# Layer 3's norm taken by halves of the channels, with a first job that begins on the upper half, and another order in layer 0's opening

## The chip, the cores and the metric

The kernel runs on one core of a Trainium2 chip. The metric is the device time of one launch in microseconds (us), the median of several runs. All data is float32.

## The reference

An image of 1024 channels and 64 x 64 pixels (one batch element) passes four residual layers, each on a group norm of its input (32 groups of 32 channels):

```python
x = x + L0(_gn(x))   # per channel: layer norm over the pixels, then a scan along the channels
x = x + L1(_gn(x))   # 1x1 convolution: weight (1024 x 1024) @ x + bias
x = x + L2(_gn(x))   # three 1x1 projections with silu, a depthwise convolution, two selective scans
                     # along sorted pixel orders, y * silu(gate) + res, an output projection, silu
x = x + L3(_gn(x))   # 1x1 convolution: weight @ x + bias
```

Layer 0, with `xn` the layer norm of its input over the pixels of each channel: `dt = softplus(sum over columns of xn * dt_w + dt_b)`, the decay of a row is `exp(-exp(log_A) * dt)`, and `out[t] = decay[t] * out[t-1] + xn[t]` along the 1024 channels. The group norm of a layer needs the mean and variance of all pixels of a group, so no pixel of a layer can be normalized before the last pixel of the layer before is there. It does not need the other channels' statistics.

## The kernel before

Pixels are cut into 8 blocks of 512 (`nb`), channels into 8 tiles of 128 (`ct`). TensorE does the 1x1 convolutions, VectorE takes statistics (`bn_stats` per tile and block, `bn_aggr` over the blocks of a tile), evicts products from PSUM and forms differences, ScalarE normalizes with `activation(Identity, scale, bias)`, POOL (GpSimd) forms sums and differences in SBUF.

A group norm is `moments` (the aggregation) followed by the generator `norm_steps`: a small matmul `pg` that averages the means over the groups, the squared deviations `d` on VectorE, a second small matmul `pv`, then `rsqrt` (Ln and Exp on ScalarE, three steps on VectorE) and the bias. It yields where one engine has to wait for another, so that the caller can put other work there. `finish_of` runs it to its end. Both small matmuls take a PSUM tile of the tag `tp`, of which there are two.

**Layer 0** works in 8 units of 2 channel tiles and half of the pixels (`u`), in 4 chunks of 2 units (one norm for each chunk, `norm_chunk`), and each unit in 4 pieces (`i`, 32 in all). For each piece: `normalize` (ScalarE), `turn_in` (TensorE transposes, evicted with scale and bias by VectorE or ScalarE according to `share`), `row_dt` (TensorE: the sums for dt into the bank `pd`), then `scan` (VectorE), `hand_on` (last column kept for the next channels), `turn_back` (transposes) and `add_up` (VectorE adds into the image and sums). `decay(u, 0..2)` makes the factors `a` of a unit: four activations, one VectorE addition, one activation. `squares` takes the next layer's variance on ScalarE. `unit_stats` takes the input's statistics. All engines follow the order written in the program (`manual_schedule`): an opening by hand, then a loop over the 32 pieces in which pieces are turned in seven ahead (`LEAD`); `todo` says in which iteration which unit's statistics are taken. `make_scores` prepares the pixel scores for the sort that layer 2 needs; it runs on VectorE ahead of the first statistics. `bring` loads the units on SP's queue, `sums` prepares weights on POOL.

**Layer 2's gate and output projections and layer 3** are matrix products in two levels of a Strassen-Winograd scheme: a job (one weight matrix, a pair of pixel blocks) has 7 outer steps `P1` to `P7` of 7 inner products each, 49 products of 8 matmuls. In `two_steps` everything is placed in slots; slot n of a job stands behind its n-th product in each engine's order. The products of two neighbouring outer steps alternate, so a step stretches over 13 slots:

```python
for slot in range(min(at), max(max(at), end + 6) + 1):
    step, i = divmod(slot, 7)
    if i % 2 == 1:
        step -= 1
    if 0 <= step < 7 * len(jobs):
        j, s = divmod(step, 7)
        outer = orders[j][s]
        product(j, outer, ("P1", "P5", "P2", "P4", "P6", "P3", "P7")[i])
    for f in at.get(slot, ()):
        f()
```

`b11`, `b12` are the upper 512 channels of the pair's first and second block, `b21`, `b22` the lower 512; `fetch` loads them on ScalarE's DMA queue, `fill` normalizes them, `comb` makes the differences t1 = b12 - b11, t2 = b22 - t1, t3 = t2 - b11, t4 = b21 - t2, and `inner_sum` the same inside a block on POOL. `SIDES` names the operand of each step: P1 takes b11, P5 t1, P2 b21, P6 t2, P7 t3, P4 t4, P3 b22. The results are C (upper channels, first block), Q (lower, second), V (lower, first) and Z or D (upper, second). `emit` adds each inner product into them, on VectorE or as a copy on ScalarE; products share PSUM banks of the tags `a`, `b7` and `b23`, two banks each. Weights come on SP's queue through `wq` (10 tiles).

Before, there are two calls of `two_steps` with a full norm between them, so the first layer-3 job (order A: P1, P2, P6, ...) begins after the statistics of all channels:

```python
    two_steps([job for pair in range(NP) for job in (("gate", WG, pair), ("out", WO, pair))], norm2, x1_d)
    nc.scalar.preload_act_table_set("natural_log_exp_and_others")
    norm3 = group_norm("gn3")
```

## Time and profile before

| | |
|---|---|
| median of 3 runs | 2768.85 us (2766.1 to 2771.12) |
| profiled execution | 2769.34 us, of which 2767.6 us span |
| granted TensorE clock, mean | 0.981 |
| first scan of layer 0 | 48.65 us from the span's start |
| first product of layer 1 | 229.28 us |
| last layer-2 product begins | 2401.75 us |
| first layer-3 product begins | 2416.68 us |

In a row of the timeline, the first number is the start in us, the second the length; then engine, line of the kernel, operation, the tile written and the tiles read, shape, and how many instructions were merged; in brackets the idle time before and what ended it. PE is TensorE, DVE VectorE, ACT ScalarE, POOL GpSimd, SP the queue that issues loads. A row of the waits gives the total in us, the number of waits and the longest. A row of busy times by stretch gives the stretch, its length, busy us of PE, PE's weight loads, DVE, ACT and POOL with the number of instructions, the granted clock, the share of the DMA engines and GB/s.

### The profile page before, as it was taken

The numbers are of one execution on the slowest core, as the hardware profiler recorded it, in microseconds if no ns is written. First come the engines' busy times: TensorE is split into PE (matmuls) and PEld (weight loads), VectorE is DVE, ScalarE is ACT, GpSimd is POOL, SyncE is SP. The second block draws the span as 40 slices with busy tenths as digits, with TensorE's granted clock in tenths as the row PEclk, the third lists the DMA queues.
The fourth block names the chain that finished last, engine by engine and source line by source line (L and its number), as shares of the span: only waits on it lengthen the run. The fifth ranks groups of instructions, "written<-read, shape, count | busy, mean of one in ns | idle before, by whom it ended". The sixth has DMA issues, their size and how long they took to land.

```text
span 2767.6 us, 30985 instructions
## 1 busy us (share of the span) xinstructions
PE 2617.4 (95%) x9586; PEld 1728.1 (62%) x9586; DVE 1771.5 (64%) x3773; ACT 1089.5 (39%) x1838; POOL 1300.5 (47%) x1175
## 2 busy tenths in 40 slices
PE   5778999999999999999999999999999999799998
PEld 4564444444555555444444446888888888688887
DVE  6986866464454564466666565577575676767777
ACT  4783110104655654465757554322233132221220
POOL 4154323421213002467686864565565566454544
PEclk9998999999999999999999999999999999899999
DMA  7345467735533434677777876889899898788896
GB/s 283 119 150 196 141 235 249 231 118 192 161 115 101 149 116 110 174 238 221 219 212 215 240 201 192 241 245 292 222 292 266 240 291 232 250 268 296 292 330 213
DMA packets 423578, 591.47 MB, mean 214 GB/s; under 512 B 149973, under 2 KB 211541, under 8 KB 420342
## 3 DMA queue, kind: packets, MB, share of 16 engines
q1 hardware_dynamic: 297110, 362.09, 41.9%
q10 hardware_dynamic: 93568, 140.52, 14.5%
q0 software_dynamic: 32736, 86.88, 12.3%
q8 instruction: 78, 1.28, 0.2%
q14 instruction: 86, 0.70, 0.1%
HBM read 432.02 MB, written 157.36 MB: 213 GB/s over the span
## 4 chain that ended last, share of the span: by engine, by line
PE 49%; POOL 3%; DMA 3%; DVE 3%; issue 1%; ACT 1%; SPq 0%; DVEq 0%; POOLq 0%; ACTq 0%
PE mm L791 9%; PE q_P5P L1547 5%; PE q_P3P L1547 5%; PE q_P7P L1547 5%; PE q_P6P L1547 5%; PE q_P4P L1547 5%; PE q_P1P L1547 5%; PE q_P2P L1547 4%; PE pg L1213 2%; PE py L1230 2%; DMA qD<-x_d 1%; POOL s L430 1%; POOL t L749 1%; PE pr L1189 1%; DMA g<-tok_d,src 0%
## 5 line engine op out<-in xcount | busy, mean ns | idle before, releaser
L791 PE MATMUL mm<-t,w 128*128 128x512 f32 x1536 | 682.8, 595 | 0.0
L791 PE MATMUL mm<-b,w 128*128 128x512 f32 x1152 | 516.9, 600 | 5.4 <-ACT b L875 4.8
L791 PEld LDWEIGHTS mm<-t,w 128*128 128x128 f32 x1536 | 286.3, 190 | 326.2 <-issue 320.7
L791 PEld LDWEIGHTS mm<-b,w 128*128 128x128 f32 x1152 | 217.4, 192 | 257.4 <-issue 246.8
L1516 ACT COPY qQ<-q_P5P 128x512 f32<-128x512 f32 x48 | 28.1, 586 | 328.1 <-PE q_P5P L1547 321.8
L980 DVE SCALAR_TENSOR_TENSOR cvp<-xs,par,cvp 128x512 f32<-128x512 f32 x128 | 95.4, 754 | 84.2 <-ACT cvp L977 81.9
L1007 POOL TENSOR_TENSOR acc<-l2xt,acc 128x136 f32<-128x136 f32 x56 | 27.8, 496 | 246.8 <-ACT l2xt L1001 243.5
L430 POOL TENSOR_TENSOR s<-s 128x256 f32<-128x256 f32 (+3 forms) x120 | 128.7, 1079 | 7.8
L1344 ACT ACTIVATE qb<-x_x_b,gn_bias,gn_r_r 128x512 f32<-128x512 f32 x128 | 96.8, 805 | 82.6 <-DVE qQ L1479 32.3
L1239 POOL DMA_INDIRECT y_d<-y,dst x74 | 75.1, 1014 | 114.4 <-ACT y L1235 48.3
L1233 ACT COPY g<-py 8x512 f32<-8x512 f32 x146 | 83.8, 574 | 111.1 <-PE py L1230 109.7
L1221 DVE TENSOR_TENSOR E<-E,pg 128x512 f32<-128x512 f32 x74 | 50.8, 687 | 109.9 <-PE pg L1213 105.2
L749 POOL TENSOR_TENSOR t<-b,t 128x512 f32<-128x512 f32 x72 | 94.2, 1335 | 55.9 <-DVE t L749 55.8
L889 DVE SCALAR_TENSOR_TENSOR image<-mm,par,image 128x512 f32<-128x512 f32 x64 | 47.2, 746 | 106.6 <-PE mm L791 106.6
L1031 DVE TENSOR_TENSOR xs<-mm,xs 128x512 f32<-128x512 f32 x64 | 41.7, 684 | 114.8 <-PE mm L791 114.8
L999 PEld LDWEIGHTS l2pt<-both,cv 128*128 128x128 f32 x512 | 77.0, 191 | 35.6 <-issue 25.6
L1547 PE MATMUL q_P1P<-t_b,wq_P1P 128*128 128x256 f32 x384 | 92.2, 385 | 6.6 <-issue 6.6
L1340 POOL TENSOR_TENSOR t_t<-qt 128x512 f32<-128x512 f32 x23 | 29.6, 1288 | 142.1 <-DVE qt L1340 80.6
L1547 PE MATMUL q_P4P<-t_t,wq_P4P 128*128 128x256 f32 x384 | 91.5, 381 | 4.9 <-issue 2.8
L1340 POOL TENSOR_TENSOR t_t<-qt,t_t 128x512 f32<-128x512 f32 x46 | 69.7, 1516 | 51.4 <-DVE qt L1340 51.1
L1547 PE MATMUL q_P2P<-t_b,wq_P2P 128*128 128x256 f32 x384 | 92.2, 384 | 0.0
L875 ACT ACTIVATE b<-image,gnl_bias,gnl_r_r 128x512 f32<-128x512 f32 x48 | 36.8, 808 | 137.4 <-DMA s<-in_w_dram 58.5
(380 smaller groups left out, 5990.1 us busy)
## 6 DMA issues: line engine op xcount, KB each, us to landing
w<-s_d SPq DMA_DIRECT2D x96, 512.0 KB, 4.3
w<-in_w_dram SPq DMA_DIRECT2D x72, 512.0 KB, 3.9
x_x_b<-x_d ACTq DMA_DIRECT2D x32, 1024.0 KB, 6.5
image<-x_d SPq DMA_DIRECT2D x12, 2048.0 KB, 12.0
wq_P6P<-s_d SPq DMA_DIRECT2D x84, 256.0 KB, 4.7
wq_P7P<-s_d SPq DMA_DIRECT2D x84, 256.0 KB, 6.3
wq_P5P<-s_d SPq DMA_DIRECT2D x84, 256.0 KB, 4.8
wq_P3P<-s_d SPq DMA_DIRECT2D x84, 256.0 KB, 4.3
```

Source lines behind the costliest of these rows:

```text
L430: eng.tensor_tensor(out, a, b, ALU.subtract)
L749: eng.tensor_tensor(B[name][k], B[one][k], B[two][k], ALU.subtract)
L791: nc.tensor.matmul(to[o], w[:, k, o * P : (o + 1) * P], B[name][k], start=(fresh and k == 0), stop=(k == KH - 1), skip_group_check=True)
L980: nc.vector.scalar_tensor_tensor(cv, xo[:, at + t : at + t + FB], pcol("dww", 3 * o + t), cv, ALU.mult, ALU.add)
L999: nc.tensor.matmul(pt[:, q * NV : (q + 1) * NV], cv[:, (q0 + q) * P : (q0 + q + 1) * P], both[:, o, :], start=True, stop=True)
L1213: nc.tensor.matmul(pg, bts, cd.rearrange("p s t -> p (s t)"), start=True, stop=True)
L1230: nc.tensor.matmul(py, G2[k % 2], rows.pop(k)[:, :DH], start=True, stop=True)
L1233: nc.scalar.copy(rows[k + 1][h * LC : h * LC + S, :DH], py[h * LC : h * LC + S])
L1239: nc.gpsimd.indirect_dma_start(out=y_d[:, :], out_offset=bass.IndirectOffsetOnAxis(ap=dst_[:, k : k + 1], axis=0), in_=y[:, :], in_offset= ...
L1340: eng.tensor_tensor(to, a, b, ALU.subtract)
L1344: nc.scalar.activation(tile_of(j, name)[:, k], held[j, "x", name][:, k], AF.Identity, bias=norm[1][:, ct : ct + 1], scale=norm[0][:, ct : ...
L1547: nc.tensor.matmul(ps[:, o, :], w[:, k, o * P : (o + 1) * P], rhs[:, k, :], start=(new and o == 0 and k == 0), stop=(k == 1), skip_group_c ...
```

## The change

For layer 3: one call of `two_steps` takes all jobs. The last layer-2 job places, beside its own work, the norm of the upper channels from slot 44 (`begin` is the ScalarE table set and the aggregation of 4 tiles, four steps at 46, 46, 47 and 47, the end at 48) and that of the lower channels from slot 56. `norm_steps` yields once more for it (`finer`). The statistics of Q move from slots 46, 47, 49, 50 to 49 to 52. The first layer-3 job gets the order D, which begins with P1 and P5, the steps that need only upper channels; its fetches, fills, combinations and the results of C move to other slots, and t4 gets a tile of its own.

For layer 0: `make_scores` yields between its steps; 18 of them stay ahead of the statistics, the others go between the steps of the first chunk's norm. The four normalizations of the first unit follow each other, pieces 0 and 1 are evicted by VectorE alone, pieces 1 and 3 are transposed into the banks of the tag `pb`. The statistics of units 2 and 3 and most of the second chunk's norm move ahead of the first scan. In the loop, `decay` 1 and 2 move ahead of `add_up`, and the statistics and norms of later chunks begin one iteration earlier and go on by one step in each.

```diff
+ORDER_D = ["P1", "P5", "P2", "P6", "P7", "P4", "P3"]
...
+        if finer:
+            yield
         pv = ps_tp(f"{name}_pv")
...
-        make_scores()
...
+        scores = make_scores()
...
+        score(18)
         for u in (0, 1):
             unit_stats(u, range(8))
-        finish_of(norm_chunk(0))
-        normalize(0)
-        normalize(1)
-        unit_stats(2, range(8))
-        turn_in(0, (1, 3))
-        normalize(2)
-        turn_in(1, (1, 3))
+        chain = norm_chunk(0)
+        for _ in range(3):
+            next(chain)
+            score(4)
+        finish_of(chain)
+        for n in range(4):
+            normalize(n)
+        unit_stats(2, range(4))
+        turn_in(0, range(4))
+        turn_in(1, range(4), "pb")
...
         row_dt(0)
-        normalize(3)
         turn_in(2, (1, 3))
         row_dt(1)
-        turn_in(3, (1, 3))
+        turn_in(3, (1, 3), "pb")
         row_dt(2)
+        unit_stats(2, range(4, 8))
+        unit_stats(3, range(4))
         row_dt(3)
-        unit_stats(3, range(4))
         decay(0, 0)
         normalize(4)
+        unit_stats(3, range(4, 8))
+        chain = norm_chunk(1)
         decay(0, 1)
         decay(0, 2)
+        next(chain)
         normalize(5)
         turn_in(4, ())
+        next(chain)
         row_dt(4)
+        next(chain)
...
-                9: [(7, range(4))], 10: [(7, range(4, 8))], 11: [(6, range(4))], 12: [(6, range(4, 8))]}
+                8: [(7, range(4))], 9: [(7, range(4, 8))], 10: [(6, range(4))], 11: [(6, range(4, 8))]}
...
             if i == 0:
-                unit_stats(3, range(4, 8))
-                finish_of(norm_chunk(1))
+                finish_of(chain)
+                chain = iter(())
+            if g == 3 and u + 1 < NU:
+                decay(u + 1, 1)
+                decay(u + 1, 2)
             if i > 0:
                 add_up(i - 1)
...
-            if i in (4, 12):
-                chain = norm_chunk(2 if i == 4 else 3)
-            if i in (6, 14):
-                finish_of(chain)
+            if i in (3, 11):
+                chain = norm_chunk(2 if i == 3 else 3)
             next(chain, None)
...
+        orders[turning - 1 : turning + 1] = ORDER_C, ORDER_D
...
+        def next_norm(s0):
+
+            for row, slot in ((0, 44), (1, 56)):
+                steps = {}
+
+                def begin(row=row, steps=steps):
+                    nc.scalar.preload_act_table_set("natural_log_exp_and_others")
+                    steps[0] = norm_steps(f"gn3_{row}", *moments(f"gn3_{row}", row * KH, KH), KH, finer=True)
...
+                then(s0 + slot, begin)
+                for i in (2, 2, 3, 3):
+                    then(s0 + slot + i, go_on)
+                then(s0 + slot + 4, end)
...
-                for name, row, col, slot, when in (("b11", 0, 0, -25, -14), ("b12", 0, 1, -14, -3),
-                                                   ("b21", 1, 0, -10, -1), ("b22", 1, 1, 1, 8)):
+                for name, row, col, slot, when in (
+                        (("b11", 0, 0, -7, -1), ("b12", 0, 1, -3, 2), ("b21", 1, 0, 3, 11), ("b22", 1, 1, 8, 14))
+                        if order is ORDER_D else
+                        (("b11", 0, 0, -25, -14), ("b12", 0, 1, -14, -3), ("b21", 1, 0, -10, -1), ("b22", 1, 1, 1, 8))):
                     on(slot, fetch, src_d, pair, row, col, (j, "x", name))
                     for k in range(KH):
-                        on(when + k, fill, j, name, row, col, k)
+                        on(when + (k // 2 if when == -1 and order is ORDER_D else k), fill, j, name, row, col, k)
...
+                if order is ORDER_D:
+                    late = [(2, "t1", "b12", "b11"), (16, "t2", "b22", "t1"), (20, "t3", "t2", "b11"), (27, "t4", "b21", "t2")]
+                    put_in = {0: -1, 1: 5, 2: 13, 3: 19, 4: 24}
...
-                done = (("C", 0, 0, {0: 27, 1: 28, 2: 29, 3: 30}), ("Q", 1, 1, {2: 46, 3: 47, 0: 49, 1: 50}),
+                done = (("C", 0, 0, {0: 27, 1: 28, 2: 29, 3: 30}), ("Q", 1, 1, {2: 49, 3: 50, 0: 51, 1: 52}),
...
-        two_steps([job for pair in range(NP) for job in (("gate", WG, pair), ("out", WO, pair))], norm2, x1_d)
-        nc.scalar.preload_act_table_set("natural_log_exp_and_others")
-        norm3 = group_norm("gn3")
-    with tc.manual_schedule(engines={E_.DVE, E_.PE, E_.Pool, E_.Activation}):
-        two_steps([("last", W3, pair) for pair in range(NP)], norm3, x2_d)
+        two_steps([job for pair in range(NP) for job in (("gate", WG, pair), ("out", WO, pair))]
+                  + [("last", W3, pair) for pair in range(NP)], norm2)
```

## The prediction

> **What bounds the kernel now.** I read the page first, then the chain of waits, then the two places that the diff touches: the seam between the last layer-2 job and the first layer-3 job (chain and PE timeline), and layer 0 (who VectorE waited for, and busy time by stretch).
>
> ```profile
> span 2767.6 us, 30985 instructions
> PE 2617.4 (95%) x9586; PEld 1728.1 (62%) x9586; DVE 1771.5 (64%) x3773; ACT 1089.5 (39%) x1838; POOL 1300.5 (47%) x1175
> PE   5778999999999999999999999999999999799998
> ```
>
> TensorE is the bound almost everywhere. Its row of tenths has two holes: the first four slices (layer 0, some 230 us) and one slice near the end. In the hole near the end the chain of waits leaves TensorE:
>
> ```profile
> 2378.75 1.74 PE q_P7P L1547 x8
> ...
> 2391.47 0.61 DVE qD L1483
> ...
> 2410.50 1.90 DVE gn_mv L179 x8
> ...
> 2415.61 0.18 DVE gn_bias L211
> ...
> 2418.88 1.27 POOL t_b L1340
> ...
> 2425.38 3.69 PE q_P1P L1547 x16
> ```
>
> For 45 us the end is set by VectorE: evictions, residual adds, statistics, then the whole norm of layer 3, and only then the first operand fill. The same place on TensorE:
>
> ```profile
> 2390.67 1.89 PE L1547 MATMUL q_P4P<-t_t,wq_P4P 128*128 128x256 f32 x8
> 2394.64 1.99 PE L1547 MATMUL q_P4P<-t_t,wq_P4P 128*128 128x256 f32 x8 [2.08 <-DVE qV L1524]
> 2399.41 2.55 PE L1547 MATMUL q_P4P<-t_t,wq_P4P 128*128 128x256 f32 x8 [2.77 <-issue]
> 2401.75 3.04 PE L1547 MATMUL q_P4P<-qQ,wq_P4P 128*128 128x256 f32 x8
> 2412.44 0.60 PE L193 MATMUL gn_pg<-gn_mv,cst 128*128 128x8 f32 x2 [7.66 <-DVE gn_mv L179]
> 2416.68 5.90 PE L1547 MATMUL q_P1P<-qb,wq_P1P 128*128 128x256 f32 x16 [2.39 <-ACT qb L1344]
> 2425.38 3.69 PE L1547 MATMUL q_P1P<-t_b,wq_P1P 128*128 128x256 f32 x16 [2.80 <-issue]
> ```
>
> A product (8 matmuls) takes 1.73 us in the steady stretch. From 2392.4 to 2425.4, 33.0 us, TensorE finishes five products, 8.6 us of work: 24.4 us are lost here. That is the most that this part can give. In layer 0, VectorE's waits and busy times:
>
> ```profile
> DVE gn_r_t L170 <- ACT gn_r_r L168: 8.8, 4, 4.3
> DVE xt L591 <- ACT a L583: 6.4, 6, 2.1
> DVE gn_d L196 <- PE gn_pg L193: 6.1, 2, 5.7
> ...
> 48.60:65.60 17.00, 14.40 (x60) 11.64 (x60) 9.98 (x27) 12.73 (x24) 7.21 (x8) 0.71 0.18 65
> ...
> 149.00:189.00 40.00, 35.03 (x215) 28.70 (x214) 35.92 (x76) 39.08 (x74) 19.26 (x32) 1.00 0.45 159
> 189.00:222.80 33.80, 18.27 (x84) 14.14 (x83) 32.30 (x69) 20.39 (x42) 17.28 (x24) 0.65 0.66 239
> ```
>
> The third and fourth busy columns are VectorE and ScalarE. VectorE is full for most of the layer and at its end; ScalarE is full from 149 to 189. VectorE's waits are the norm's round trips (5.7 for the sums on TensorE, 3.5 and 4.3 for Ln and Exp on ScalarE) and the decay factors `a`. Layer 1 begins when this layer ends, so what is saved here reaches the end.
>
> **The seam, walked through.** Slots are products of 1.73 us; slot 49 of the last layer-2 job is slot 0 of the first layer-3 job. Until slot 44 nothing differs, so the last statistics of D end at 2392.8 as they do now. VectorE's queue then gets four aggregations (eight take 1.97, so 1.0) and is at 2393.8. TensorE has finished slot 46 at 2389.0 and must take the norm's first small matmul next: it waits 4.8 us there, in front of slots 47 and 48. Matmul 0.6, slot 47 until 2396.1, second matmul until 2396.8 (the three small VectorE steps that it needs end at 2396.1, behind slot 45's and 46's evictions), Ln and Exp, four VectorE steps of 0.2, norm of the upper half at 2400.0, two fills of 0.8: the first layer-3 product runs from about 2401 to 2403, where it now starts at 2416.7. Slot 1 (a left-over P4 product) covers 1.7. Slot 2 needs fills 2 and 3, which stand on ScalarE behind the eviction of slot 0, a table load and one Silu: 0.57+1.28+0.72+1.6 after 2403.1, so 2407.3: about 2 us of stall. Slots 3 to 8 then run without a gap until 2418.9. VectorE meanwhile has its old work (16 adds and statistics of Q and V, 10 us) and four combs for t1 (2.8): comb 3 ends at 2420.1, so slot 9 waits 1.2; V's statistics end at 2422.7, four aggregations at 2423.7, and the second norm's first matmul, queued after slot 9, waits 1.8 more. Its scale is there at about 2428.4, the fills of b21 at 2430.6; slot 14, the first product that needs them, starts at 2431.9. Now it starts at 2441.2 (seven products before and seven after it run without a hole). Gain 9.3.
>
> What the walk leaves out is the clock. In the trace, the granted clock after the 7.7 us gap is 0.50 (both norm matmuls and the first P1 product), and after the 2.8 us gap it is 0.77 and then 0.66 (2.55 and 3.04 us for a product of 1.73). The Trainium skill, "TensorE: Matmul & The Clock Gate" (The HAM clock gate), says that the clock halves after an idle window of about 3.4 us and needs as long of work to return. Row and rule differ for the short gap: by the rule alone it should not have slowed anything. They agree that the new 4.8 us wait at slot 46 will: some 3.4 us at half speed, 1.7 us of work lost. It speaks against this change, which puts that wait where TensorE now runs at full clock (without it, 9.3; with it, 7.6). I take it, and for the wait on ScalarE's issue of fetches, which the walk counted at 3 us and the trace shows overlapped now, give back 0.9: **8.5 us**.
>
> The sets of ScalarE: now one switch at 2410.2, after the last Silu. With the norm at slot 44 it is ln/exp, Silu again at slot 49, ln/exp at 56: two more. The trace has 1.28 us for a load; the skill, "ScalarE: Activation LUTs" (What ACT_TABLE_LOAD costs), gives 2.66 with the drain. Only the load in front of slot 2 is on the path: 1.28 is in the walk, by the page's price slot 2 is 1.4 later and the gain 7.1. I stay with the trace: the first activation after 2410.2 waits for VectorE, so the drain is not seen either way; both ends are in the range.
>
> At nothing I cost: Q's move from slots 46-50 to 49-52 (VectorE has D before it), the shorter lead of the fetches (xq has four buffers, fetches land in 6.5 us, b21 is issued near 2413 and needed at 2429; if it came late, each us is a us), the new tile for t4, and the other order of steps in this job: in 2425-2510 VectorE is busy 61.0 of 85 us, POOL 44.3, ScalarE 18.6, and the job does the same products. If that slack were not at the right slots, a hole costs what it lasts. SP's weight loads keep their order and stay ten tiles ahead. Bounds of this part: 2 (TensorE waits for both norms in full, at half clock) and 16 (no wait after the first product).
>
> **Layer 0.** Counted from the first norm's end (27.5). Before it: 16 of 22 score steps stay ahead of the statistics, six and the transpose go into the norm's round trips. Statistics could start near 10.6, not 12.9; but the second unit's block (issued at 4.93, 12.1 us to landing, so 17.0) is used from 17.7, so at most 0.7 is won; the steps put into the chain delay it by about as much (a copy that waits for the score transpose stands before `gn_v`). Net 0, bounds -1 and +1.5.
>
> Then the order. Now: first scan 48.65, second 65.60, with VectorE idle 5.7 us in between. Changed: all four normalizations first (4.9 on ScalarE), pieces 0 and 1 evicted by VectorE (four more evictions of 0.49), two pieces in the "pb" banks, so piece 1's transposes don't wait for evictions. The row sums start 0.8 earlier. But 7.4 us of statistics and the second chunk's norm now stand on VectorE before the first scan: m at 48.9, aggregation until 50, the second matmul of that norm behind piece 4's transposes, the first scan near 53.5 instead of 48.65. In return the norm's last steps follow the first scan at once: second scan near 61.8 instead of 65.6. From there TensorE's turn_back, behind ScalarE's evictions, decides: ScalarE's evictions of pieces 5 to 7 come some 1 us later than now (it waits for m before it may write `a`), so the first add-up comes 1.4 to 3.6 us earlier. I take 2, bounds -4 and +5.
>
> Chunks 2 and 3: the chain starts one iteration earlier and goes one step at a time, so that Ln and Exp lie a whole scan before their use. The 3.5 and 4.3 us go. ScalarE is idle 5 of 20 us around the first and 5 of 15 around the second, so some of it turns into waits for ScalarE: 2.5 and 3. The factors `a`: decay steps 1 and 2 move ahead of add-up and evictions. Of 6.4 us, the first scan's 1.07 is in the opening; 2.12 lies where ScalarE is full and gains nothing; of the other 3.2 I take half of the 1.48 before 189 and nearly all of the small ones: 1.5 with rounding down. Sum 2+2.5+3+1.5 = 9; ScalarE's full 40 us (149 to 189) must also start earlier for this to count, which it does only as far as TensorE lets it: I take **7.5**, bounds 0 and 13. Shorter layer 0 also pulls together the weight loads at 205-225 (DMA share 0.7 to 1.0), which cover nothing critical: the first layer-1 product waits for the fill.
>
> **Sum.** 7.5+8.5 = 16. The profiled execution took 2769.34 (span 2767.6 and 1.7 around it), so 2753.3; the median of the three runs shown is 0.5 below that: 2752.9, say 2753.
>
> **Rivals.** (1) The seam closes fully: VectorE catches up while TensorE works on the upper half, no second wait. For it: 14 products, 24 us, lie between first product and first need of the lower half. Against: VectorE was 5.3 us behind at slot 44 already. 15+9: 2745. (2) The wait moves instead of going: small matmuls in TensorE's queue wait for VectorE's backlog twice, at half clock. For it: the walk's 4.8 and 1.8. 3+7 = 10: 2759. (3) Layer 0 is ScalarE's: its later start eats what VectorE saves. 0+8: 2761. (4) Slower, one mechanism: the first scan's delay. The second chunk's norm matmul stands behind piece 4's transposes at half clock; if row sums and transposes of pieces 4 to 6 all run at 0.50 (the trace has 0.50 at 51-55), each costs 1.7 more, ScalarE follows, and layer 0 ends 5 us later than now, while the seam gives 2: 2772. It decides from where the second scan comes later than 67.6 (two us over now's 65.6, the seam's lower bound); VectorE's slack speaks against it. (5) It doesn't do what it says: the layer-3 products wait for the lower half all the same, and layer 0 is neutral: 2767.
>
> **Numbers.** Likeliest case 0.50; (1) 0.20; (2) 0.18; (3) 0.07; (4) 0.03; (5) 0.02. A difference under 0.2% (5.5 us) is about what a measurement here cannot tell from none; the border is 2763.3. Faster by more: all of the first two, nearly all of (2) and most of (3), 0.92; within 0.05; slower 0.03. The range takes (1)'s 2745 with 4 us for the bounds of layer 0, and (3) with the page's dearer table loads: 2741 to 2763.
>
> **What would show it.** Right: PE rows near 2376-2430 (shifted by layer 0) where P1 products of the layer-3 job alternate with P4; one gn_pg wait of 4 to 5 us and a second under 2; three table loads; the aggregation as two groups of four; the first-to-second scan gap near 8, not 17; no Ln wait over 1 us for VectorE. Wrong: a gap over 5 us before the P2 products of that job, holes inside it, or layer 1 beginning no earlier than 229.

## The result, and the profile after

The changed kernel takes 2760.76 us, the median of 10 runs (2757.49 to 2764.36), beside 2770.47 us for 10 runs of the kernel before: a ratio of 0.9965, 95% interval 0.9955 to 0.9974. That is 9.7 us, where 16 were forecast; the time lies in the range.

From the page of the changed kernel, the span, the busy times and the TensorE row of tenths:

```profile
span 2759.0 us, 31019 instructions
PE 2619.3 (95%) x9590; PEld 1728.2 (63%) x9590; DVE 1777.6 (64%) x3785; ACT 1090.0 (40%) x1838; POOL 1303.5 (47%) x1175
PE   4788999999999999999999999999999999899998
```

The busy time of TensorE is the same within 2 us. The hole near the end has gone from a 7 to an 8: it is shallower, not closed.

**The seam.** TensorE's timeline of the changed kernel, the same place as before:

```profile
2392.25 0.59 PE L194 MATMUL gn_pg<-gn_mv,cst 128*128 128x4 f32 x2 [4.73 <-DVE gn_mv L180]
2392.70 3.76 PE L1620 MATMUL q_P7P<-qC,wq_P7P 128*128 128x256 f32 x8
2396.25 0.43 PE L203 MATMUL gn_pv<-gn_d,cst 128*128 128x4 f32 x2
2396.54 2.27 PE L1620 MATMUL q_P4P<-t_t,wq_P4P 128*128 128x256 f32 x8
2401.09 2.27 PE L1620 MATMUL q_P1P<-qb,wq_P1P 128*128 128x256 f32 x8 [2.29 <-ACT qb L1388]
...
2406.76 2.27 PE L1620 MATMUL q_P1P<-qb,wq_P1P 128*128 128x256 f32 x8 [1.68 <-ACT qb L1388]
...
2420.99 1.56 PE L1620 MATMUL q_P5P<-qb,wq_P5P 128*128 128x256 f32 x6 [1.09 <-DVE qb L1384]
2424.96 0.39 PE L194 MATMUL gn_pg<-gn_mv,cst 128*128 128x4 f32 x2 [2.41 <-DVE gn_mv L180]
2425.21 1.97 PE L1620 MATMUL q_P1P<-t_b,wq_P1P 128*128 128x256 f32 x8
```

Before, TensorE had six waits here, 18.4 us in all, the longest 7.66 us in front of the norm. Now it has five, of 4.73, 2.29, 1.68, 1.09 and 2.41 us, 12.2 in all. The first P1 product begins at 2401.09 where it began at 2416.68, and P1 products of the layer-3 job alternate with left-over P4 products. A full-speed product has a row of 1.89 here (its last end is modelled); the one behind the first wait has 3.76. The chain of waits in the same stretch:

```profile
2391.23 0.97 DVE gn_mv L180 x4
2392.84 3.62 PE q_P7P L1620 x8
...
2403.99 1.28 ACT L1552
2405.28 0.73 ACT qQ L1552
2406.03 0.70 DVE qQ L1554
...
2423.95 0.97 DVE gn_mv L180 x4
```

VectorE still sets the end up to the second aggregation at 2423.95, except for two pieces: the slow product at 2392.84, which the norm's second small matmul stands behind, and the load of the Silu table with one Silu at 2403.99, for which VectorE stands idle 5.84 us.

**Layer 0.** VectorE's waits in the first 225 us, then the busy times of the stretch in which ScalarE was full before, then TensorE's timeline at the start of layer 1:

```profile
DVE low L640 <- PE pb L630: 3.2, 1, 3.2
...
DVE xt L616 <- ACT a L608: 2.2, 3, 1.0
...
DVE gn_r_t L171 <- ACT gn_r_r L169: 0.5, 1, 0.5
```

```profile
149.00:189.00 40.00, 36.26 (x218) 30.67 (x219) 36.21 (x75) 39.52 (x74) 20.36 (x32) 1.00 0.47 171
```

```profile
224.07 16.34 PE L828 MATMUL mm<-b,w 128*128 128x512 f32 x31 [2.39 <-ACT b L912]
```

The 8.8 us of waits for Ln and Exp are 0.5, those for the factors `a` fell from 6.4 to 2.2. New is the wait of the first add-up for TensorE's transposes, 3.2. Layer 1 begins 5.2 us earlier. ScalarE (the fourth busy column) is full from 149 to 189 as it was.

To follow a gain through the execution I use a *lead*: the start of a row of VectorE, less the start of the same row in the profile of before (below zero is earlier). The seam's own gain is the lead of the rows near 2350, ahead of it, less the lead of those near 2500, behind it. For the changed kernel these are -1.59 and -8.57: the seam gained 7.0 us.

### The profile page after: what moved, and what is told of

It reads as the page before. It is cut to its first block, busy times and chain, and to the rows that moved or that the text cites. A ratio compares the mean times of both kernels' runs of the same rounds, so it can differ in the third digit from the quotient of the medians.

```text
span 2759.0 us, 31019 instructions
## 1 busy us (share of the span) xinstructions
PE 2619.3 (95%) x9590; PEld 1728.2 (63%) x9590; DVE 1777.6 (64%) x3785; ACT 1090.0 (40%) x1838; POOL 1303.5 (47%) x1175
## 3 DMA queue, kind: packets, MB, share of 16 engines
q0 software_dynamic: 32736, 86.88, 12.2%
q8 instruction: 78, 1.28, 0.2%
## 4 chain that ended last, share of the span: by engine, by line
PE 50%; DMA 3%; POOL 3%; DVE 3%; issue 1%; ACT 1%; DVEq 0%; POOLq 0%; ACTq 0%
PE mm L828 10%; PE q_P7P L1620 5%; PE q_P5P L1620 5%; PE q_P3P L1620 5%; PE q_P6P L1620 5%; PE q_P4P L1620 5%; PE q_P1P L1620 4%; PE q_P2P L1620 4%; PE pg L1250 2%; PE py L1267 2%; DMA qD<-x_d 2%; DMA g<-tok_d,src 1%; POOL s L457 1%; PE pr L1226 1%; POOL t L786 0%
## 5 line engine op out<-in xcount | busy, mean ns | idle before, releaser
L1620 PE MATMUL q_P5P<-t_t,wq_P5P 128*128 128x256 f32 x384 | 90.8, 379 | 0.0
```

The costliest lines, as they stand in the source:

```text
L1620: nc.tensor.matmul(ps[:, o, :], w[:, k, o * P : (o + 1) * P], rhs[:, k, :], start=(new and o == 0 and k == 0), stop=(k == 1), skip_group_c ...
```

## The experiments

All ratios are against runs of the kernel before on the same chip. In the profile of before, layer 1 begins at 229.28; the kernel with the seam's part alone has the same layer 0 and 227.94, and the changed kernel has 224.07 and 225.07 in two profiles. So a difference of 1 us in that column says little.

| kernel | median us | ratio, 95% interval | layer 1 begins | seam's gain |
|---|---|---|---|---|
| changed | 2760.76 | 0.9965 [0.9955, 0.9974] | 224.07 | 7.0 |
| layer 0's part alone | 2767.94 | 0.9993 [0.9985, 1.0001] | 224.50 | 0.0 |
| seam's part alone | 2764.46 | 0.9982 [0.9973, 0.9991] | 227.94 | 4.9 |
| four fills first | 2761.39 | 0.9969 [0.9959, 0.998] | 224.31 | 3.0 |
| Silu ahead | 2756.0 | 0.9951 [0.9934, 0.9969] | 224.28 | 8.8 |
| norm's steps later | 2756.53 | 0.9954 [0.994, 0.9967] | 224.75 | 8.9 |
| Silu ahead, steps later | 2753.86 | 0.9936 [0.992, 0.9953] | 224.23 | 11.2 |
| the same, joint table set | 2753.19 | 0.9944 [0.993, 0.9957] | 224.44 | 11.8 |
| opening alone (seam changed) | 2761.38 | 0.9972 [0.9962, 0.9982] | 226.32 | 7.7 |
| decays as before | 2763.46 | 0.9975 [0.9964, 0.9986] | 226.25 | 6.8 |
| chains as before | 2762.16 | 0.9978 [0.9971, 0.9986] | 225.18 | 5.3 |
| waits filled | 2761.89 | 0.9967 [0.9954, 0.9979] | 224.73 | 6.7 |
| changed, once more | 2761.76 | 0.9959 [0.9943, 0.9975] | 225.07 | 5.4 |

### The two parts apart

The first kernel has the diff's layer-0 hunks alone (`make_scores` to the loop over the pieces), the second all the others.

> Layer 0's part of the change alone, the seam before layer 3 as in the kernel before. In the changed kernel layer 1 begins 5.2 us earlier, but of that 1.4 us is left when the first product of the last two layers' jobs begins (1686.14 before, 1684.73 changed). Theory A (the lead of layer 0 is partly lost in layer 2's scan stretch, 1116 to 1680, whose chain goes over indirect loads, POOL and weight stores): first product of layer 1 at 224 +- 0.5, time 1 to 4 us below the kernel before (ratio 0.9986 to 0.9996). Theory B (the lead carries in full, the loss in the one profile was chance): 5 us, ratio 0.998. Rival C (all of it is lost there, the stretch keeps its own clock): ratio 1.000, and the first product at 1686.

> The seam's part alone, layer 0 as before. Theory: what the profile shows between the seventh step of the last layer-2 job and the first product on lower channels is the seam's own, 7.0 us (slot 14 at 2432.6 against 2441.2, less the 1.6 us of lead it came with): 7 us below the kernel before, ratio 0.9975, and with theory A of the other run the two parts add up to the measured 9.7 us. Rival: the seam depends on what comes in ahead of it (its waits shift with DMA phase), then 4 or 10 us.

By time, layer 0's part is worth 0.07% (1.9 us, its interval reaches from 4 us to nothing), the seam's part 0.18% (5 us). Together they come to 6.9 of the 9.7 us, which is within the intervals. So less than half of layer 0's 4.8 us at the start of layer 1 (229.28 to 224.50) is seen in this time; added to the seam's part, the same hunks are worth more (0.9982 against 0.9965, 4.7 us). The lead in that profile is -4.8 at 401, -3.8 at 495, -2.5 from 680 to 1080 and -1.7 at 1120.

In the seam alone the waits are those of the changed kernel, but the products are not. TensorE's timeline:

```profile
2395.84 3.76 PE L1586 MATMUL q_P7P<-qC,wq_P7P 128*128 128x256 f32 x8
...
2399.68 2.94 PE L1586 MATMUL q_P4P<-t_t,wq_P4P 128*128 128x256 f32 x8
2404.92 3.66 PE L1586 MATMUL q_P1P<-qb,wq_P1P 128*128 128x256 f32 x8 [2.29 <-ACT qb L1354]
```

The second and third product take 2.94 and 3.66, where the changed kernel's profile has 2.27 and 2.27. The waits add up to 12.15 us against 12.20, yet the seam gains 4.9 instead of 7.0. The size of the clock's loss is thus a term of its own, and the part on why comes back to it. (The 2.27 at 2401.09 does not come from the clock: the granted clock is 1.00 there, and part of the product stands until ScalarE's second fill ends.)

### What holds the 1.68 and 2.41 us waits

Theory V: VectorE's own queue of adds and statistics sets when the second norm begins. Theory S: the order on ScalarE (fills behind table load and Silu) does. First, all four fills of b11 go ahead of Q's Silu:

```diff
-                        on(when + (k // 2 if when == -1 and order is ORDER_D else k), fill, j, name, row, col, k)
+                        on(when + (0 if when == -1 and order is ORDER_D else k), fill, j, name, row, col, k)
```

> The changed kernel with fills 2 and 3 of b11 placed on ScalarE ahead of Q's first Silu and its table load. Theory S (every stall of TensorE at the seam is its own): the 1.68 us wait of the second P1 product goes, 1.5 to 1.7 us faster than the changed kernel (ratio to the kernel before 0.9959). Theory V (VectorE's chain through Q's and V's statistics to the second norm is the bound, and TensorE's early waits are slack): Q's Silu comes 1.5 us later, so VectorE idles 7.3 instead of 5.84 us, the second norm's small matmul waits 1.5 us more than its 2.41 and the time is that of the changed kernel within 0.5 us (0.9965).

From TensorE's timeline:

```profile
2404.43 1.89 PE L1620 MATMUL q_P1P<-qb,wq_P1P 128*128 128x256 f32 x8
...
2414.57 1.56 PE L1620 MATMUL q_P5P<-qb,wq_P5P 128*128 128x256 f32 x6 [0.91 <-DVE qb L1384]
...
2423.34 0.59 PE L194 MATMUL gn_pg<-gn_mv,cst 128*128 128x4 f32 x2 [2.40 <-DVE gn_mv L180]
2423.78 3.76 PE L1620 MATMUL q_P1P<-t_b,wq_P1P 128*128 128x256 f32 x8
```

The 1.68 us wait is gone (the second P1 product has no bracket), a new one of 0.91 has come, and the norm waits 2.40 as before: TensorE arrives earlier and waits for VectorE elsewhere. The time is the changed kernel's. VectorE now stands idle 7.24 us for Q's Silu, as V said; the norm's longer wait that V expected did not come, since TensorE came later itself, slowed by its clock. Then Q's Silu itself goes ahead, so that VectorE need not stand idle for it (Q's Silus at their old places fall away):

```diff
+            def silu_q(j, k, o):
+                c = tile_of(j, "Q")[:, k]
+                nc.scalar.activation(c, c, AF.Silu, bias=pcol("bout", o))
...
+                if order is ORDER_D:
+                    for k in (3, 0):
+                        on(-1, silu_q, j - 1, k, KH + k)
...
-("Q", 1, 1, {2: 49, 3: 50, 0: 51, 1: 52}),
+("Q", 1, 1, {2: 49, 3: 49, 0: 49, 1: 50}),
...
+                    if quick and kind == "out" and name == "Q" and k in (1, 2):
+                        on({2: 48, 1: 50}[k], silu_q, j, k, o)
```

> The changed kernel with the Silu table load and Q's first Silu placed in ScalarE's 1.9 us wait for the end of the first norm, two further Silus right behind the first two fills, and Q's adds and statistics on VectorE from slot 49 to 50. Theory V: VectorE's 5.84 us of idle shrinks to 1 to 2 us, V's statistics end 3 to 4 us earlier, the waits of 1.68, 1.09 and 2.41 us go nearly all: 4 us faster than the changed kernel, ratio to the kernel before 0.995. Theory S: only the first wait (1.68) goes, ratio 0.9959. Rival: the Silu delays the first fill by more than it saves: 0.9965 or above.

TensorE's timeline has three waits left, one of 4.71 at the first group sum and these two:

```profile
2402.29 3.64 PE L1630 MATMUL q_P1P<-qb,wq_P1P 128*128 128x256 f32 x8 [2.29 <-ACT qb L1388]
...
2423.87 0.39 PE L194 MATMUL gn_pg<-gn_mv,cst 128*128 128x4 f32 x2 [2.20 <-DVE gn_mv L180]
```

The waits of 1.68 and 1.09 are gone and 9.2 us are left. The ratio is 0.0014 (3.9 us) under the changed kernel's, though the two intervals overlap. VectorE's idle time for Q's Silu is 0.86 instead of 5.84. This speaks for V: VectorE's queue is what runs late, and the table load in front of its work was part of the reason. But the norm still waits 2.20: what VectorE won, TensorE won too.

### The norm's steps two slots later

```diff
-                for i in (2, 2, 3, 3):
+                for i in (4, 4, 4, 4):
```

> The changed kernel with the steps of both half-norms two and one slots later in the last layer-2 job (go_on counts 4,4,4,4 in place of 2,2,3,3), so that TensorE runs slots 47 and 48 before it waits for the aggregated statistics, and the same for the second norm. Theory C (TensorE's queue and clock: a product that could run stands behind the 4.7 us wait, and the wait halves the clock): the gn_pg wait falls from 4.73 to 1 to 2 us, the first P7P product after it runs at 2 to 2.5 us instead of 3.76, the upper half's norm ends 0 to 1.6 us earlier, and the seam is 1.5 to 3 us shorter: ratio about 0.9957 against the changed kernel's 0.9965, in the profile the first P2 product 1.5 to 3 us earlier counted from the first P1 product's predecessors. Theory V (VectorE's own queue decides when the statistics are there and TensorE's waits only move): the wait shrinks by the two products moved ahead, the waits of 2.29, 1.68, 1.09 and 2.41 grow by as much, and the time is the changed kernel's, 0.9965.

TensorE's timeline:

```profile
2395.28 0.39 PE L194 MATMUL gn_pg<-gn_mv,cst 128*128 128x4 f32 x2 [1.27 <-DVE gn_mv L180]
2399.27 0.59 PE L203 MATMUL gn_pv<-gn_d,cst 128*128 128x4 f32 x2 [3.60 <-DVE gn_d L199]
2402.22 3.78 PE L1620 MATMUL q_P1P<-qb,wq_P1P 128*128 128x256 f32 x8 [2.37 <-ACT qb L1388]
```

Now slots 47 and 48 run ahead of the wait, at full speed. The 4.73 becomes 1.27, but six evictions stand on VectorE between the aggregation and `gn_d`, and TensorE waits 3.60 for that. The second norm finds its statistics there at once and waits 1.03 for its `gn_d`. In all 10.05 us of waits instead of 12.2. The ratio, 0.0011 (3 us) under the changed kernel's, is what C expected, though the two intervals overlap. But the slow product has not gone: it is now the first P1, with 3.78, which C did not expect.

### Both together, and the table set

> Both at once: Q's Silu and its table load ahead of the norm's end (the earlier run: the waits of 1.68 and 1.09 gone, ratio 0.9951) and the norm's steps later (the run beside this one). If the two take different losses away, the gains add: with theory C some 5 us under the changed kernel, ratio 0.994 to 0.995. If VectorE's queue is the one limit behind both, no more than the earlier Silu alone gives: 0.9951.

ScalarE's timeline shows a cost that the Silu put ahead has brought in:

```profile
2394.72 1.28 ACT L168 ACT_TABLE_LOAD   x1
2397.68 0.20 ACT L168 ACTIVATE gn_r_r<-gn_v 128x4 f32<-128x4 f32 x1 [1.67 <-DVE gn_v L211]
2397.90 1.28 ACT L169 ACT_TABLE_LOAD   x1
```

The set loaded for Ln does not hold Exp, so a second load of 1.28 us stands between the two, with VectorE waiting. The next kernel names the joint set behind that Silu:

```diff
                 nc.scalar.activation(c, c, AF.Silu, bias=pcol("bout", o))
+                if k == 2:
+                    nc.scalar.preload_act_table_set("natural_log_exp_and_others")
```

> The kernel with Q's Silu ahead and the half-norms' steps later (ratio 0.9936 so far), and a load of the joint ln/exp set behind the Silu that goes ahead. There the trace showed the set changed for Ln at 2394.72 (hidden) and once more for Exp at 2397.90, 1.28 us on the path between Ln and Exp of the first half-norm. With the joint set loaded instead, Ln and Exp need no second load: theory P (the load is on the path): the wait of the first P1 product falls from 3.64 to 2.3 to 2.4, the seam is 1.3 us shorter, ratio near 0.993. Theory H (the load lies beside VectorE's backlog and only the order of waits changes): the same time as without it, 0.9936, with another wait longer by 1 us or more.

Its ScalarE timeline:

```profile
2393.34 0.20 ACT L168 ACTIVATE gn_r_r<-gn_v 128x4 f32<-128x4 f32 x1 [1.67 <-DVE gn_v L211]
2393.58 0.20 ACT L169 ACTIVATE gn_r_r<-gn_r_r 128x4 f32<-128x4 f32 x1
```

Exp now follows Ln at once, and the first P1 product waits 2.36 instead of 3.64, as P said. The seam gains 11.8 instead of 11.2, and not the 1.3 more that P said: the product behind P1 took 3.00 instead of 2.35, which gave half of it back. By time the two kernels cannot be told apart. Silu ahead gave the seam 8.8, later steps 8.9, both 11.2, which looks as if the two added; but each is one profile, and beside the Silu alone the pair has the same waits (9.17 after 9.20 us) and only faster products. With the joint set the waits fall as well, to 7.88. That the two add is likely and not shown. Without the joint set the pair takes 0.9936 [0.992, 0.9953] of the time before. That is faster than the kernel before, and some 6 to 8 us under the changed kernel: the interval lies just under that of its first runs (0.9965 [0.9955, 0.9974]) and overlaps that of its second (0.9959 [0.9943, 0.9975]).

### Layer 0, piece by piece

Three kernels keep the changed seam and undo parts of layer 0. "Opening alone" has the loop as before, "decays as before" only puts `decay` back behind the add-up, "chains as before" only the norms and statistics of chunks 2 and 3:

```diff
-            if i in (3, 11):
-                chain = norm_chunk(2 if i == 3 else 3)
+            if i in (4, 12):
+                chain = norm_chunk(2 if i == 4 else 3)
+            if i in (6, 14):
+                finish_of(chain)
```

> The changed kernel with layer 0's loop as before (chains of chunks 2 and 3 begun at pieces 4 and 12 and forced to their end at 6 and 14, statistics one piece later, decay steps after the add-up); its opening and the seam stay as changed. Layer 1's first product began at 229.28 before and at 224.07 with the change: 5.2 us. By the prediction's terms the opening alone is worth 2 of 9, so layer 1 would begin near 228; if, as the trace after reads, the second scan's 6.7 us earlier start is given back only in part by scan 6 (1.9 left), it begins at 227 to 227.5, and the two chains and the decays hold the other 3 to 3.5. If the loop's part is swallowed by ScalarE's full stretch from 149 to 189, it begins at 224.5 to 225. Ratio 0.997 to 0.998.

> The changed kernel with the steps of the decay factors alone put back behind the add-up and the evictions. The prediction gives them 1.5 us: layer 1 begins near 225.5, with VectorE waiting 3 to 5 us in all for the factors a (2.2 in three waits with the change, 6.4 in six before). If ScalarE, which is full from 149 to 189, gives it back, layer 1 begins at 224.1 to 224.6 as with the change. Ratio 0.9965 to 0.997, not to be told apart by time; the profile decides.

> The changed kernel with only the norms of chunks 2 and 3 in layer 0 as before (begun at pieces 4 and 12, forced to their end at 6 and 14, statistics of chunks 2 and 3 one piece later); the opening, the decays and the seam stay as changed. So far layer 1's first product began at 229.28 before, 224.07 with all of the change, 226.32 with the opening alone, 226.25 without the decays. Theory A (the three terms add: 3.0 opening, 2.2 decays, chains 0): layer 1 begins at 224.1 here. Theory B (chains and decays are worth nothing one by one and 2.2 together, since the wait taken from the norm comes back as a wait for the factors a: VectorE waited 8.6 us for them without the decays' move, 2.2 with it): it begins at 226 to 226.4. The prediction's terms (chains 5.5) would give 229. Ratio 0.9965 to 0.9975, not to be told apart by time; the profile decides.

VectorE's waits in the first 225 us for the factors `a` and for Ln and Exp, with the opening alone:

```profile
DVE gn_r_t L171 <- ACT gn_r_r L169: 7.6, 3, 3.6
DVE xt L616 <- ACT a L608: 4.5, 5, 2.1
```

With the decays as before (opening and chains changed):

```profile
DVE xt L616 <- ACT a L608: 8.6, 5, 3.2
...
DVE gn_r_t L171 <- ACT gn_r_r L169: 0.5, 1, 0.5
```

With the chains as before (opening and decays changed):

```profile
DVE gn_r_t L171 <- ACT gn_r_r L169: 7.3, 3, 3.5
...
DVE xt L616 <- ACT a L608: 0.4, 1, 0.4
```

By the start of layer 1, the opening alone gives 3.0 us against the profile of before (226.32 after 229.28), 1.6 against the other profile with the old layer 0. Added to the opening, the chains alone give 0.1 (226.25) and the decays alone 1.1 (225.18). Both together give 1.3 to 2.3 in the nine profiles with all of layer 0's part, which begin layer 1 at 224.07 to 225.07. The 1.1 of the decays are beyond that spread by little, so whether the chains add anything to them cannot be told; 5.5 is excluded, and so is theory B in its strict form. What is plain is the trade. With the chains alone, the waits for Ln and Exp fall by 7.1 us and those for `a` rise by 4.1. Both are results that ScalarE hands to VectorE, so a round trip taken off VectorE's path comes back as a wait for `a` unless `a` moves forward too. That ScalarE's full stretch from 149 to 189 keeps the rest is only argued: no run here lifts it.

### TensorE kept busy in its waits, and the changed kernel again

In front of the group sums stand matmuls that compute nothing:

```diff
         pg = ps_tp(f"{name}_pg")
+        if finer:
+            for _ in range({"gn3_0": 16, "gn3_1": 8}[name]):
+                nc.tensor.matmul(pg[:, :256], ident, cst[:, :256], start=True, stop=True)
```

> The changed kernel with matmuls that compute nothing used (16 of 128x256 from a constant into the tile of gn_pg, as long as two products, ahead of the first half-norm's group sum; 8 ahead of the second's), so that TensorE works through 3.5 of the 4.7 us and 1.7 of the 2.4 us that it waits in front of them. Nothing else moves. Theory C (the wait costs its clock besides its length): the product after gn_pg runs at 1.7 to 1.9 us instead of 3.76 and the next at 1.9 instead of 2.3 to 2.9, gn_pv comes 1 to 1.9 us earlier where VectorE's gn_d allows it, and the seam is 1 to 2.5 us shorter than the changed kernel's beside it, whose own length changes from profile to profile by the phase of the clock (the changed seam gained 4.9 to 7.7 us in five profiles); ratio 0.9955 to 0.996 against 0.9965. Theory V (VectorE's backlog sets gn_pv and all that follows): the products run warm, gn_pv waits for gn_d instead, the seam is the same within 0.5 us and the ratio 0.9965.

> The changed kernel once more, beside the run with the filled waits. Two things are read from it. First the scatter: with the same program, the lead of layer 0 at the end of layer 2 stood anywhere between -1.2 and -7.3 us in the profiles so far (0 is the profile of before), and the seam's gain between 4.9 and 7.7; if these are the run's and not the edits', this profile differs from the first one by 1 us or more in either of them while the waits at the seam (4.7, 2.3, 1.7, 1.1, 2.4) stay within 0.1. If they are the edits', it repeats -1.6 and 7.0 within 0.3. Second the time: 0.9965 within 0.001.

TensorE's timelines, first of the kernel with the filler, then of the changed kernel again:

```profile
2384.77 7.07 PE L196 MATMUL gn_pg<-cst 128*128 128x256 f32 x32
2391.68 0.28 PE L197 MATMUL gn_pg<-gn_mv,cst 128*128 128x4 f32 x2
2391.82 1.97 PE L1623 MATMUL q_P7P<-qC,wq_P7P 128*128 128x256 f32 x8
```

```profile
2394.00 0.59 PE L194 MATMUL gn_pg<-gn_mv,cst 128*128 128x4 f32 x2 [4.72 <-DVE gn_mv L180]
2394.44 3.76 PE L1620 MATMUL q_P7P<-qC,wq_P7P 128*128 128x256 f32 x8
...
2398.28 2.56 PE L1620 MATMUL q_P4P<-t_t,wq_P4P 128*128 128x256 f32 x8
2403.12 3.55 PE L1620 MATMUL q_P1P<-qb,wq_P1P 128*128 128x256 f32 x8 [2.29 <-ACT qb L1388]
```

The filler was mis-sized: the trace shows two instructions for each of these float32 matmuls (x32 for 16), and so a product's 8 are four matmuls of the program; 16 of them last as long as four products, 7.07 us and not 3.5. They held the group sum up by 2.0 us after the aggregation was there (it ended at 2389.61). All the same `gn_pv` followed the end of the aggregation by 4.0 us, as it did in the changed kernel (2397.99 after 2393.94), since the product between them ran at 1.97 instead of 3.76. So a wait at this place costs some 2 us beyond its length. The granted clock is 1.00 from 2384.77 to 2440 in this profile, the only one of the changed seam without a slow stretch there. The time says nothing more: 0.9967 and 0.9959 are not apart; that the overlong filler took what the full clock gave is argued from the rows.

The changed kernel's second profile has the same five waits within 0.02 us and a seam gain of 5.4 instead of 7.0, and its lead ahead of the seam is +0.2 instead of -1.6. Both differences belong to the execution and not to an edit.

## Why the prediction was right, and where its sizes were off

The time lies 2.2 us inside the range's upper edge. Both parts came out smaller than forecast, so no error made up for another; it was the width of the range that held them.

**The walk through the seam held.** The first wait was forecast at 4.8 us (4.73), the upper half's norm at 2400.0 (its first fill starts at 2400.22 in a profile with a lead of 1.6, so 1.8 later than walked, the length that the slow product adds), the stall of slot 2 at 2 (1.68), slot 9 at 1.2 (1.09), three table loads (three). The second norm's wait was put at 1.8 and is 2.41, over the limit of 2 that the prediction set itself.

**The clock was the mis-sized term.** The prediction took off 1.7 us for it, and gave 0.9 back for the issue of fetches. In the table, "slow products" adds up what the products after the first wait last beyond their row at full speed. "Of it clock" is half of the time that products ran in stretches with a granted clock of 0.50; the gain is the seam's:

| profile | waits | slow products | of it clock | gain | waits + slow + gain |
|---|---|---|---|---|---|
| changed | 12.20 | 3.36 | 2.18 | 6.98 | 22.54 |
| changed, once more | 12.19 | 4.93 | 4.07 | 5.43 | 22.55 |
| seam alone | 12.15 | 5.49 | 4.58 | 4.93 | 22.57 |
| opening alone | 12.16 | 2.79 | 1.54 | 7.71 | 22.66 |
| decays as before | 12.18 | 3.44 | 2.27 | 6.80 | 22.42 |
| chains as before | 12.20 | 5.06 | 4.21 | 5.25 | 22.51 |
| four fills first | 11.41 | 7.79 | 7.41 | 3.03 | 22.23 |
| Silu ahead | 9.20 | 4.84 | 4.36 | 8.81 | 22.85 |
| norm's steps later | 10.05 | 3.57 | 2.82 | 8.85 | 22.47 |
| Silu ahead, steps later | 9.17 | 2.43 | 2.25 | 11.19 | 22.79 |
| the same, joint set | 7.88 | 3.08 | 2.91 | 11.83 | 22.79 |

The sums come to 22.2 to 22.9 us in eleven profiles, so nothing else of size is at work there. (With the chains as before the gain is read ahead of 2550, where another 0.4 us was lost.) The first six have the changed seam and equal waits. About 1.0 us of their slow products is not the clock: in good part it is the first two P1 products, whose later matmuls stand for a fill (2.27, as also with the filler, where the clock is full). Without the clock the gain is thus 22.5 - 12.2 - 1.0 = 9.3, which is the walk's 9.3. The clock took 1.5 to 4.6 us, 3.1 on average, where 1.7 were forecast, and the 0.9 given back shows up in no run. Together they make the gain 6.2 on average instead of 8.5. The direction of the argument (the change puts a wait where TensorE runs at full clock) was right. In time, 9.7 us is nearest to rival 2, the wait that moves and is paid at half clock, which had 10.

**The clock rule.** The prediction weighed a rule of the Trainium skill, "TensorE: Matmul & The Clock Gate" (The HAM clock gate), which halves the clock after an idle window of some 3.4 us, against a row in which 2.8 us had already slowed TensorE. Behind the 4.7 us wait the next product takes 3.49 to 3.76 in all six profiles of the changed seam, as rule and row would have it. Behind the 2.4 us wait it takes 1.97 in the changed kernel and 3.76 with the four fills first. So 2.4 us can cost a full 1.9 us or nothing.

The traces show what decides. They record when the granted clock changed: within one profile all changes lie on a grid of 3.41 us, and the grid lies elsewhere in every execution. Here are two neighbouring windows of the grid around the 2.4 us wait, first in the changed kernel, then with the four fills first (the stretch, its length, TensorE's busy us and instructions, the granted clock, the share of the DMA engines, GB/s):

```profile
2421.03:2424.45 3.42, 1.53 (x6) 1.00 0.32 111
2424.45:2427.86 3.41, 2.90 (x15) 1.00 1.01 329
```

```profile
2419.67:2423.08 3.41, 1.26 (x6) 1.00 0.44 131
2423.08:2426.50 3.42, 3.16 (x9) 0.50 1.03 337
```

The grid cuts the same wait at different places. With 1.53 us of work in the first window the next one has the full clock, with 1.26 us it has half. I counted this for 19 pairs of windows from 2376 on in each of the 14 profiles. All 21 full-clock windows with at most 1.37 us of work are followed by half clock, and none of the 204 with 1.44 us or more. A window at half clock is followed by another one after 3.16 us of work or less, and by the full clock after 3.18 or more. So the window need not be idle, as the rule has it. In the kernel before, the window ahead of the row that the prediction wondered at (2397.24 to 2400.65) has 1.24 us of work. This also explains why equal waits lose 1.5 us of clock in one execution and 4.6 in another. Elsewhere in the program the border is less sharp (a window with 2.1 us of work in layer 0 was followed by half clock), so these figures hold for this seam.

**Table loads.** The sum had 1.28 us for the load on the path; the row at 2403.99 has 1.28, and the Silu begins 0.01 us behind it. The larger price of the Trainium skill, "ScalarE: Activation LUTs" (What ACT_TABLE_LOAD costs), 2.66 us with the drain, would have cost another 1.4 and is not seen here. What the walk missed is what that load does to VectorE: it stands idle 5.84 us for Q's Silu, and the kernel with the Silu ahead takes 1.68 and 1.09 us of waits away.

**Layer 0 was forecast at 7.5 and came to 5.2** (4.2 to 5.2 in the nine profiles that have all of it, against the profile of before; 2.9 to 3.9 against the seam alone, which has the old layer 0 too). By terms: the opening 2, measured 1.6 to 3.0; the two chains 2.5 and 3, measured 0.1 to 1.1 in all according to what stands beside them; the decays 1.5, measured 1.1 to 2.2. The opening's scans came at 53.34 and 58.91 where 53.5 and 61.8 were worked out. The step that failed is the one that counted the chains' 5.5 as nearly free of ScalarE: of 7.8 us of waits it took 2.3 off for what ScalarE could not do earlier, and another 1.5 off the sum for ScalarE's full stretch from 149 to 189. That is rival 3 in part.

**Whether layer 0's gain reaches the end stays open.** The prediction said that "what is saved here reaches the end". Against the profile of before, the mean lead of the nine profiles with all of layer 0's part shrinks from -4.8 at the start of layer 1 to -2.6 at 1120 (-1.4 to -4.0). The traces show three places where that happens. Around 488 TensorE waits for a tile of the sort, 0.91 us in the profile of before and 0.88 to 1.89 in the nine, and in each of them the lead changes by that difference. Behind the norms at 620 and 1090 TensorE runs at half clock for one or two windows of the grid; this costs 2.0 and 1.7 us before and 1.4 to 2.9 and 1.7 to 2.7 in the nine, and again the lead changes by the difference, within 0.1 us. But the seam alone, with the old layer 0, waits 1.92 and loses 2.3 and 2.4 at these places. So the loss is read off one execution of the kernel before that was short there: against the seam alone the mean lead is -3.4 at the start of layer 1 and -3.6 at 1120. Through layer 2's scan stretch, from 1120 to 1666, the lead of the nine changes by -4.2 to +2.6 us with no edit there, and at 1666 they stand between -1.2 and -7.3. In time, layer 0's part is worth 1.9 us alone and 4.7 beside the seam's part, which does not decide it either.

## What to carry to other kernels

When a wait cannot be removed, look at which queue it stands in and at what speed the engine runs before and after it: here the same statistics cost about 2 us more because two ready products stood behind the small matmul, and putting those two first, with the next layer's Silu ahead of the norm, was worth nearly as much again at the seam as the change itself (11.2 us in one profile, beside a mean of 6.2). A round trip that is hidden for one engine comes back as a wait for another result of the same helper engine unless that engine has idle time there, so read its waits after the edit as a sum. A gain at the start of a long program should be followed by its lead to the end, and against more than one profile of before: here 2 us of lead seemed to go, and it was one execution's shorter stalls. And where the clock is at stake, ask how much work each window of its grid holds, not how long a wait is.

## What the runs showed of the hardware that was not expected

- All changes of the granted clock within one profile lie on a grid of 3.41 us, and at this seam 1.37 us of work or less in a window brings half clock in the next, 1.44 us or more does not (14 profiles).
- The granted clock after equal waits differs between executions of one program: behind a 4.72 us wait the first product takes 3.76 us both times, the next one 2.27 in one profile and 2.56 in the other; the one after that runs at full clock in the first and takes 3.55 in the second.
- A gap of 2.4 us cost a product nothing (1.97 us) in one kernel and doubled it (3.76 us) in another.
- A table set loaded for Ln did not serve Exp: a second load of 1.28 us stood between them.
- Executions of one program drift apart by several us: nine profiles whose kernels do not differ ahead of the seam have leads from -1.2 to -7.3 us at 1666, and one and the same kernel has -1.6 and +0.2 us just ahead of the seam. So the span of one profile cannot rank edits of this size.
